# A front that reads x twice instead of turning and normalizing it, with 23 of 36 convolution taps as matmuls

## The chip, the cores and the metric

The kernel runs on one core of one Trainium2 chip. The metric is the device time of one execution in microseconds (us). Before the change three runs took 2659.55, 2660.99 and 2661.44 us; the median, 2660.99 us, is the time before.

## What is computed

Four layers follow each other on an image batch x of 2 x 512 x 32 x 32 in float32. The change touches the beginning of the first layer only, a deformable attention:

```python
xn = _bn(x, bn1_g, bn1_b)                       # x * s + b, per channel
q = _gconv1x1(xn, qw)                           # 8 groups of 64 channels
off = conv_general_dilated(qg, off_dw_w, (4, 4), ((1, 1), (1, 1)), ...)   # depthwise, 6 x 6 = 36 taps
off = gelu(off + off_dw_b)
off = tanh(einsum(off, off_pw_w)) * 4.0         # two offsets for each of 8 x 8 positions
vgrid_scaled = ...                              # positions moved by the offsets
kv = _grid_sample(xn, vgrid_scaled)             # bilinear samples, 0 outside the image
k = _gconv1x1(kv, kw)
v = _gconv1x1(kv, vw)
pos = grid_q - grid_kv                          # every pixel against every sampled position
bias = sign(pos) * log1p(abs(pos))
bias = relu(bias @ cpb_w1 + cpb_b1)             # 2 -> 128
bias = relu(bias @ cpb_w2 + cpb_b2)             # 128 -> 128
bias = (bias @ cpb_w3 + cpb_b3)                 # 128 -> 1
attn = softmax(qh kh + bias); out = attn vh     # then a projection, an MLP, and three more layers
```

There are 2 images x 8 groups of 64 positions and 1024 pixels. The kernel takes two groups (128 channels) at a time as a chunk k = 0..3, and one image of one chunk as g = 0..7. Position j of both groups of a g is a "key": 512 keys in all, n = 0..511.

## The kernel before

**Front (lines 367 to 618).** It loads x channel by channel into four tiles `xn[k]` (128 channels x 2048 pixels, 1 MB each) and makes everything that the first key needs. For chunk 0: `normed_` (VectorE) scales and shifts x, `query` (TensorE, line 421) multiplies by the query weights `qw`, `queried` (ScalarE, line 426) copies the result to `q` in another pixel order. 36 taps follow: 21 on VectorE (`Chain.tap`, lines 229 and 232) and 15 as matmuls with diagonal weights (`taps_pe`, lines 372 and 519; the diagonals are made on VectorE and GpSimd, line 451). Line 535 adds the two sums. Then `gelu`, `offsets`, `tanh`, `position`, `size`, `log`, `sign`, `feature` make a table of sign * log for the 64 positions; for the first eight keys matmuls spread it over all partitions (`pfb`, line 568) and `tab_scale` (line 174) makes the table `tab`. `turn`, `turned` and `put` store the table to DRAM (`fd`, line 331), from where `tab_load` (line 162) reads it for all later keys, eight at a time.

The same front also makes q for chunks 1 to 3 (`norm` on ScalarE or `normed_` on VectorE, `query`, `queried`), and turns the normalized x: `flip_x` (TensorE transposes, line 437) and `flipped` (copies, line 438) write it with pixels on partitions into `xt`, a view of the big tile `x`. The samples need it in that form.

**Order.** After `started.append(0)` every instruction that is wrapped in `pin` stays in program order on its engine. The order of the front is therefore written out by hand. Loads go out on SP's queue (`nc.sync`) and, at the start, on ScalarE's.

**Loop over keys (lines 972 to 985).** For each pair of keys p and each quarter o of 32 hidden units, `second` (line 649) runs eight matmuls into `ph`, one of two PSUM buffers, and ScalarE's relu (line 658) empties it. `first` (VectorE, line 355) makes the input `h1` of key n + 2, `combine` (VectorE, line 664) joins two quarters. `h1` has four buffers. All other work is put between these by a plan: `at(n, when, fn)` runs fn after quarter 0/2 or 1/3 of key n. `prepare(g)` samples: `hat`, `hat2` (ScalarE) and `cross` (VectorE) make bilinear weights from the coordinates `co`, `sample` (TensorE, line 738) multiplies them with `xt`, `got` (VectorE, line 749) copies the samples to `kv`. `attend(g)` does the softmax of an earlier g. `chain(k0, k1, n, taken)` repeats the front's work from the taps to `put` for chunk 1 (ending at key 85) and for chunks 2 and 3 together (ending at key 213), with all taps on VectorE.

Of the kernel before, what the change touches and what calls it, by code (L numbers as in the profile page):

```python
# [56 lines left out]
_CONSTS = [("ident", P), ("grid", 2 * J), ("gridf", J), ("npx", 1), ("npy", 8), ("sel3", 2)]  # L57
# [15 lines left out]
def conv_seq(  # L73
    ctx: ExitStack,
    tc: tile.TileContext,
    x_in: bass.AP,
    vecs: bass.AP,
# [24 lines left out]
    xt = x.rearrange("p k n -> p (k n)").rearrange("p (t c) -> p t c", c=C)  # L102
# [32 lines left out]
    with ExitStack() as ctx_l0:  # L135
# [66 lines left out]

        class Chain:
# [79 lines left out]

# [81 lines left out]
        with tc.tile_pool(name="a", bufs=1) as a, tc.tile_pool(name="aps", bufs=5, space=PSUM) as aps, tc.tile_pool(  # L367
            name="apc", bufs=1, space=PSUM
        ) as apc, tc.tile_pool(name="apk", bufs=1, space=PSUM) as apk:


            taps_pe = [(1, 2), (1, 3), (1, 4)] + [(ky, kx) for ky in (0, 5) for kx in range(6)]
            diag = a.tile([P, len(taps_pe), P], F32, name="diag")
            xn = [a.tile([P, NT], F32, name=f"xn{k}") for k in range(KC)]
            qw = a.tile([P, KC, P], F32, name="qw")
            ordc = a.tile([P, NORDER], F32, name="ordc")
            nc.scalar.dma_start(qw[:, 0], qkv_w[:, 0, 0])
            nc.scalar.dma_start(cst, consts)
            nc.scalar.dma_start(qw[:, 1:], qkv_w[:, 0, 1:])
            for t in range(NT // 512):  # L380
                b, half = divmod(t, 2)
                nc.sync.dma_start(xn[0][:, t * 512 : (t + 1) * 512], x_dram[0][:, b, half * 512 : (half + 1) * 512])
            for k in range(1, KC):
                nc.sync.dma_start(xn[k].rearrange("p (b n) -> p b n", b=B), x_dram[k])
                if k == 1:
                    nc.sync.dma_start(offw, off_w)
                    nc.sync.dma_start(cpbw, cpb_w)
                    nc.sync.dma_start(ordc, order)
            nc.sync.dma_start(kvw, qkv_w[:, 1:3])
            nc.sync.dma_start(wo, out_w)  # L390
            started.append(0)
            pqs, pts = {}, {}
# [4 lines left out]
            for _ in range(9):  # L397
                pin(nc.tensor.matmul(pidle, lhsT=idle, rhs=idle, start=True, stop=True))


            def norm(k):
                pin(
                    nc.scalar.activation(
                        xn[k], xn[k], AF.Identity, bias=v("L0_conv_bn1_b", k), scale=s12[:, 0, k : k + 1]
                    )
                )

            def normed_(k, *ts):
                for t in ts:
                    xs = xn[k][:, t * 512 : (t + 1) * 512]  # L410
                    pin(
                        nc.vector.tensor_scalar(
                            xs, xs, s12[:, 0, k : k + 1], v("L0_conv_bn1_b", k), ALU.mult, ALU.add
                        )
                    )

            def query(k, *ts):
                for t in ts:
                    pqs[k, t] = aps.tile([P, 512], F32, name="pq", tag="p")
                    rhs = xn[k][:, t * 512 : (t + 1) * 512]  # L420
                    pin(nc.tensor.matmul(pqs[k, t], lhsT=qw[:, k, :], rhs=rhs, start=True, stop=True))

            def queried(k, *ts):
                for t in ts:
                    pin(
                        nc.scalar.copy(
                            q[:, k, t * 512 : (t + 1) * 512].rearrange("p (y c x) -> p y c x", c=4, x=SIDE),
                            pqs.pop((k, t)).rearrange("p (y x c) -> p y c x", c=4, x=SIDE),
                        )
                    )  # L430

            def flip_x(k, t, copy):

                pt = aps.tile([P, 4, P], F32, name="pt", tag="p")
                for i in range(4):
                    at = (4 * t + i) * P
                    pin(nc.tensor.transpose(pt[:, i], xn[k][:, at : at + P], ident))
                pts[k, t] = lambda: pin(copy(xt[:, 4 * t : 4 * t + 4, k * P : (k + 1) * P], pt))

            def flipped(k, *ts):  # L440
                for t in ts:
                    pts.pop((k, t))()
# [9 lines left out]

            act, dve = nc.scalar.copy, nc.vector.tensor_copy
# [44 lines left out]
            ch = Chain(0, 1, lambda shape, name: apc.tile(shape, F32, name=name, tag="c"))  # L498
            for t in range(NT // 512):
                normed_(0, t)  # L500
                query(0, t)
                queried(0, t)
                if t == 1:
                    signs()
                elif t == 2:
                    diagonals(0, 2, nc.vector)
            diagonals(2, 7, nc.vector)
            diagonals(7, len(taps_pe), nc.gpsimd)
# [4 lines left out]
            flip_x(0, 0, act)  # L513
            flip_x(0, 1, act)
# [13 lines left out]
            flip_x(0, 2, act)  # L528
            flip_x(0, 3, act)
            flipped(0, 0, 1)  # L530
            norm(1)
            flipped(0, 2, 3)
            query(1, 0, 1, 2, 3)
            queried(1, 0, 1, 2)
# [3 lines left out]
            for i, m in enumerate(("below", "same")):  # L538
                pin(nc.tensor.matmul(pcnt[:, i : i + 1], lhsT=oc(m), rhs=pos, start=True, stop=True))
            ch.offsets()  # L540
# [3 lines left out]
            normed_(2, 0, 1)  # L544
            ch.position()
            flip_x(1, 0, act)
            flip_x(1, 1, act)
            ch.spread(0)
            flip_x(1, 2, act)
            flip_x(1, 3, act)  # L550
            ch.size()
            ch.log()
            ch.sign()
            normed_(2, 2)
            ch.coordinate(0)
            normed_(2, 3)
            ch.feature()
            counted()
            queried(1, 3)
            flipped(1, 0)  # L560

            tab0 = tabs[0] = tabp.tile([P, TK, 2, 64], F32, name="tab")
            for u0 in range(0, 8, 4):
                pfb = apk.tile([P, 4, 2, 64], F32, name=f"pfb{u0}")
                for u in range(4):
                    key = u0 + u
                    pin(
                        nc.tensor.matmul(
                            pfb[:, u].rearrange("p a f -> p (a f)"),
                            lhsT=ch.feat[:, key : key + 1].to_broadcast([P, P]),  # L570
                            rhs=ident,
                            start=True,
                            stop=True,
                        )
                    )
                for ax in range(2):
                    pin(tab_scale(tab0, ax, u0, u0 + 4, pfb))
                if u0 == 0:
                    flipped(1, 1, 2)
            first(0)  # L580
# [5 lines left out]
            flipped(1, 3)  # L586
            query(2, 0, 1)
            pw2 = apk.tile([P, P], F32, name="pw2", tag="pfb0")
            pin(nc.tensor.matmul(pw2, lhsT=cpbw, rhs=perm, start=True, stop=True))
            placed()  # L590
            first(1)
            norm(3)
            query(2, 2, 3)
            ch.spread(1)
            queried(2, 0, 1, 2, 3)
            psb = apk.tile([P, 4, 2], F32, name="psb", tag="pfb4")
# [3 lines left out]
            query(3, 0, 1)  # L600
            flip_x(2, 0, dve)
            query(3, 2)
            flip_x(2, 1, dve)
            query(3, 3)
            spread_out()
            ch.coordinate(1)
            queried(3, 0)
            flipped(2, 0)
            queried(3, 1, 2)
            flipped(2, 1)  # L610
            queried(3, 3)
            for k, t in ((2, 2), (2, 3), (3, 0), (3, 1), (3, 2), (3, 3)):
                flip_x(k, t, (dve, act)[t % 2])
            flipped(2, 2, 3)
            ch.column(0)
            flipped(3, 0, 1)
            ch.column(1)
            flipped(3, 2, 3)
# [8 lines left out]
        with tc.tile_pool(name="hid", bufs=3) as hid, tc.tile_pool(name="sm", bufs=1) as sm, tc.tile_pool(name="hps", bufs=2, space=PSUM) as hps, tc.tile_pool(  # L627
# [74 lines left out]
            def prepare(g):  # L702
# [28 lines left out]
                def sample():  # L731
                    pool, tag = (sps, "psim1") if own else (mps, "m")
                    ps = st["pkv"] = pool.tile([P, J], F32, name="pkv", tag=tag)
                    for t in range(8):
                        for h in range(2):
                            ch = k * P + h * DH
# [3 lines left out]
                                    lhsT=xt[:, b * 8 + t, ch : ch + DH],  # L740
# [6 lines left out]
                def got():  # L747
                    st["kv"] = smpp.tile([P, J], F32, name="kv")
                    pin(nc.vector.tensor_copy(st["kv"], st["pkv"]))
# [172 lines left out]

            def load(ch):
# [25 lines left out]
            def chain(k0, k1, n, taken):  # L949
                ch = Chain(k0, k1, lambda shape, name: mps.tile(shape, F32, name=name, tag="m"))  # L950
                for i, tap in enumerate(taps):
# [5 lines left out]
                    (10, 0, ch.sign), (11, 0, ch.feature), (11, 1, ch.column, 0), (12, 1, ch.column, 1),  # L957
                ]
                for i in range(k1 - k0):
                    plan += [(13 + i, 1, ch.turn, i), (14 + i, 0, ch.turned, i)]  # L960
                    plan += [(14 + i, 0, ch.put, i, b) for b in range(B)]
                for dn, when, fn, *args in plan:
# [3 lines left out]
            chain(2, 4, 213, 116)  # L966
# [1076 lines left out]
def _layout(a):  # L2043
# [46 lines left out]
    put("gridf", gq[:, None] + f(1.0) - f(2.0) / f(SIDE - 1) * gf)  # L2090
    put("npx", -(p % 32).astype(f)[:, None])
# [22 lines left out]
    for h in range(2):  # L2114
# [5 lines left out]
        "x": got["x"],  # L2120
        "vecs": vecs,
# [38 lines left out]
```

## Time and profile before

One execution was profiled. Its rows tell:

| what | value |
|---|---|
| the profiled execution's own time | 2659.79 us |
| its span, first to last instruction | 2658.0 us |
| around the span | 1.79 us |
| median of the three runs | 2660.99 us |
| front: span start to the first line-649 matmul | 37.38 us |
| matmuls of line 649, 16384 of them | 1770.7 us busy |
| relus of line 658, 1024 | 1141.8 us busy, 1115 ns each |
| `first` of line 355, 512 | 1169.3 us busy, 2284 ns each |
| `combine` of line 664, 512 | 653.9 us busy, 1277 ns each |
| VectorE, 37 to 787 us | 47.4 to 50.0 us busy in each 50 us |
| ScalarE, 37 to 787 us | 33.5 to 42.1 us busy in each 50 us |

A timeline row gives the start, the length, the engine, the line, the operation, "out<-in" by tile names, the shape, a count, and in brackets how long the engine had been idle and what ended it. Consecutive rows of one kind are merged, so the length of a row with x8 covers eight instructions. A float32 matmul appears as two passes, a transpose as one. In a row of stretches the busy time of each engine stands with the number of instructions, then the granted TensorE clock, the share of the DMA engines and GB/s.

### The profile page before, as it was taken

Reading aid. Unit: us, or ns where it says so; the run is one execution under the profiler, and the core shown is the slowest. Engines: PE = TensorE matmul, PEld = TensorE weight load, DVE = VectorE, ACT = ScalarE, POOL = GpSimd, SP = SyncE. Lnnn points to the kernel's source line nnn. Section 1 sums busy time; section 2 is a strip of 40 time slices with the busy share of each in tenths; the row PEclk is TensorE's granted clock in tenths of the full one; section 3 lists DMA queues with packets and bytes.
Section 4 is the critical chain, followed back from the end, with each engine's and each line's share of the span. In section 5 each row is a group of like instructions: output and inputs, shape, how many; then the busy total and the mean of one; then the engine's idle time right before and its main releaser. Section 6 shows DMA issues by size and latency. Waiting matters only on the chain.

```text
span 2658.0 us, 48892 instructions
## 1 busy us (share of the span) xinstructions
PE 2620.5 (99%) x19644; PEld 978.0 (37%) x19644; DVE 2252.6 (85%) x2042; ACT 1556.5 (59%) x2123; POOL 888.5 (33%) x1048
## 2 busy tenths in 40 slices
PE   9999999999999999999999999999999999999997
PEld 5222323333332333323232333333444444476544
DVE  7999999999999999999999999999554544648645
ACT  6777687777768777866867777777321111011334
POOL 1444444444444454444545445445200000000001
PEclk9999999999999999999999999999999999999998
DMA  4888888888888888888998899898410000010001
GB/s 138 167 165 170 167 157 161 173 159 161 172 167 157 160 178 157 164 174 160 172 199 172 158 194 177 159 177 158 101 31 24 16 24 24 16 65 1 1 1 64
DMA packets 113426, 335.08 MB, mean 126 GB/s; under 512 B 22672, under 2 KB 32400, under 8 KB 112432
## 3 DMA queue, kind: packets, MB, share of 16 engines
q0 software_dynamic: 77824, 251.72, 53.1%
q1 hardware_dynamic: 34800, 79.73, 9.0%
q8 instruction: 154, 2.52, 0.4%
q14 instruction: 72, 0.59, 0.1%
q10 hardware_dynamic: 576, 0.51, 0.1%
HBM read 58.99 MB, written 4.46 MB: 24 GB/s over the span
## 4 chain that ended last, share of the span: by engine, by line
PE 90%; DVE 5%; issue 2%; ACT 2%; DMA 0%; DVEq 0%; SPq 0%; ACTq 0%
PE ph L649 60%; PE A L1141 4%; PE D L1141 4%; PE C L1141 4%; PE B L1141 2%; PE po L1076 2%; DVE h L355 2%; DVE r L664 1%; PE pg L1339 1%; PE pscore L1649 1%; PE psim L692 1%; PE prC L1308 1%; PE prA L1308 1%; PE prD L1308 1%; PE pz L1678 1%
## 5 line engine op out<-in xcount | busy, mean ns | idle before, releaser
L649 PE MATMUL ph<-h,w2a 128*32 128x512 f32 x16384 | 1770.7, 592 | 7.5 <-ACT r L658 4.8
L658 ACT ACTIVATE r<-ph,sb 128x1024 f32<-128x1024 f32 x1024 | 1141.8, 1115 | 472.9 <-PE ph L649 453.2
L355 DVE CUSTOM_DVE_ANT_1 h<-tab 128x2048 f32<-128x2048 f32 x512 | 1169.3, 2284 | 19.1 <-PE ph L649 17.2
L649 PEld LDWEIGHTS ph<-h,w2a 128*32 128x32 f32 x16384 | 521.7, 109 | 1233.1 <-issue 769.3
L664 DVE SCALAR_TENSOR_TENSOR r<-r,rel,r 128x1024 f32<-128x1024 f32 x512 | 653.9, 1277 | 22.9 <-ACT r L658 21.6
L672 POOL DMA_DIRECT2D r<-r x512 | 473.4, 1141 | 175.5 <-DMA r<-r 164.8
L667 POOL DMA_DIRECT2D r<-r x256 | 234.7, 917 | 726.9 <-DVE r L664 617.0
L683 POOL DMA_DIRECT2D xs<-r x256 | 313.1, 1223 | 107.1 <-DMA xs<-r 83.6
L1423 POOL MEMSET M<- 128x512 f32 x2 | 1.0, 526 | 429.2 <-PE pt L1330 429.2
L174 ACT ACTIVATE tab<-tab,vec 128x256 f32<-128x256 f32 x252 | 137.6, 546 | 0.0
L1934 POOL TENSOR_TENSOR x<-x,aff 128x512 f32<-128x512 f32 x7 | 7.0, 1036 | 316.3 <-issue 316.3
L1181 ACT COPY u<-A 128x512 f32<-128x512 f32 x16 | 9.4, 586 | 146.9 <-PE A L1141 146.9
L1160 ACT ACTIVATE h<-h,vec 128x512 f32<-128x512 f32 x32 | 23.1, 721 | 113.7 <-DVE h L1163 113.7
L1163 DVE TENSOR_TENSOR h<-C,u 128x512 f32<-128x512 f32 x32 | 22.1, 690 | 48.6 <-PE C L1141 48.3
L1141 PE MATMUL A<-xn,w 128*128 128x512 f32 x128 | 60.3, 593 | 0.8 <-DVE x L1083 0.8
L1141 PE MATMUL C<-hT,w 128*128 128x512 f32 x128 | 60.3, 592 | 0.0
L1141 PE MATMUL A<-h,w 128*128 128x512 f32 x128 | 60.1, 592 | 0.0
L1201 DVE TENSOR_TENSOR x<-D,x 128x512 f32<-128x512 f32 x32 | 22.1, 690 | 25.8 <-PE D L1141 25.7
L1201 DVE TENSOR_TENSOR x<-C,x 128x512 f32<-128x512 f32 x32 | 22.1, 690 | 24.8 <-PE C L1141 24.8
L882 ACT ACTIVATE e<-e,den 128x64 f32<-128x64 f32 x128 | 42.4, 342 | 0.9 <-DVE den L878 0.9
L868 ACT ACTIVATE e<-psm,mx 128x64 f32<-128x64 f32 x128 | 39.3, 314 | 2.4 <-DVE mx L863 2.3
L1339 PE MATMUL pg<-xt 128*128 128x512 f32 (+3 forms) x128 | 36.4, 439 | 1.4 <-ACT xt L1337 1.1
(403 smaller groups left out, 1936.7 us busy)
## 6 DMA issues: line engine op xcount, KB each, us to landing
r<-r POOLq DMA_DIRECT2D x256, 512.0 KB, 5.0
r<-r POOLq DMA_DIRECT2D x256, 256.0 KB, 5.9
r<-r POOLq DMA_DIRECT2D x256, 128.0 KB, 4.7
tab<-fd SPq DMA_DIRECT2D x63, 512.0 KB, 6.4
xs<-r SPq DMA_DIRECT2D x256, 64.0 KB, 2.7
xs<-r POOLq DMA_DIRECT2D x256, 64.0 KB, 5.3
lw<-in_l_w_dram SPq DMA_DIRECT2D x5, 1024.0 KB, 9.0
x<-in_x_dram SPq DMA_DIRECT2D x4, 1024.0 KB, 12.2
```

The source lines that it names most:

```text
L174: return nc.scalar.activation(tf, tf if src is None else src[:, :, ax, :], AF.Identity, bias=0.0 if ax == 0 else v("L0_conv_cpb_b1"), scal ...
L355: nc.vector._custom_dve(TENSOR_ADD_SAT, out=h1, in0=columns.unsqueeze(1).to_broadcast([P, 32, 2, 32]), in1=rows_.unsqueeze(3).to_broadcast ...
L649: nc.tensor.matmul(ph[t * 32 : (t + 1) * 32, i, :], lhsT=w2a[:, o], rhs=h1s[2 * p + i][:, half * 16 : (half + 1) * 16, h, :], start=True, ...
L658: pin(nc.scalar.activation(r, ph, AF.Relu, bias=sb3[:, o, 1:2]))
L664: pin(nc.vector.scalar_tensor_tensor(r0, r1, rel[:, i : i + 1], r0, ALU.mult, ALU.add))
L667: pin(nc.gpsimd.dma_start(rs[p, 0], rs.pop((p, 2)), accum_op=ALU.add))
L672: pin(nc.gpsimd.dma_start(r[0 :: 2 * step], r[step :: 2 * step], accum_op=ALU.add))
L683: pin(nc.gpsimd.dma_start(xs_[t][d::8], rs.pop((p, 0))[4::8], accum_op=ALU.add))
L1076: nc.tensor.matmul(po, lhsT=(vwo, wo)[t // 2][:, k, o * P : (o + 1) * P], rhs=q[:, k, ts_], start=(k == 0), stop=(k == KC - 1),)
L1141: nc.tensor.matmul(banks[bank], lhsT=a[an][k], rhs=b_[bn_][k], start=(i < 4 and k == 0), stop=(k == n - 1), skip_group_check=True,)
L1308: nc.tensor.matmul(banks[bank], lhsT=a[an][:, k, o * P : (o + 1) * P], rhs=b_[bn_][:, k, :], start=(i < 4 and k == 0), stop=(k == 1), skip ...
L1339: nc.tensor.matmul(pgs[i], lhsT=xt[:, i * P : (i + 1) * P], rhs=xt[:, i * P :], start=(t == 0), stop=(t == 7),)
```

## The change

- x is not normalized. The scale goes into the query weights (`query_scale` makes `qws`), the shift becomes a bias of the query (`query_bias`: a one-column matmul for each chunk, copied to `qb`) that `queried` adds.
- x is not turned. A second input `x_pos` holds the raw x with pixels on partitions, laid out by the host; four loads of 1 MB put it into `xt`.
- So the samples are of raw x. `got` multiplies them by the scale and adds shift times the sum of the sample's weights, which is less than 1 at the image border. `off_middle`, `within` and `shifts` compute that sum, for all three chains.
- 23 taps instead of 15 run as matmuls; 9 diagonals are made on GpSimd, 8 on ScalarE and 6 on VectorE. VectorE keeps 13 taps.
- `size` and `sign` of the front's chain move to VectorE (`size_sign`, `signed`), the spreading matmuls become transposes, and the order of the front's instructions, the loads and the PSUM pools is new.

```diff
-            taps_pe = [(1, 2), (1, 3), (1, 4)] + [(ky, kx) for ky in (0, 5) for kx in range(6)]
+            taps_pe = [(1, kx) for kx in (2, 3, 4, 1, 0, 5)] + [(2, kx) for kx in (2, 3, 1, 0, 5)]
+            taps_pe += [(ky, kx) for ky in (0, 5) for kx in range(6)]
...
+            nc.scalar.dma_start(cst[:, 0:P], consts[:, 0:P])
             nc.scalar.dma_start(qw[:, 0], qkv_w[:, 0, 0])
-            nc.scalar.dma_start(cst, consts)
-            nc.scalar.dma_start(qw[:, 1:], qkv_w[:, 0, 1:])
...
+            nc.sync.dma_start(ordc, order)
+            nc.sync.dma_start(cpbw, cpb_w)
+            nc.sync.dma_start(cst[:, P:], consts[:, P:])
+            nc.sync.dma_start(offw, off_w)
+            nc.sync.dma_start(qw[:, 1:], qkv_w[:, 0, 1:])
             for k in range(1, KC):
                 nc.sync.dma_start(xn[k].rearrange("p (b n) -> p b n", b=B), x_dram[k])
...
+            nc.sync.dma_start(xt[:, 0].rearrange("p t c -> p (t c)"), x_pos[:, 0])
             nc.sync.dma_start(kvw, qkv_w[:, 1:3])
             nc.sync.dma_start(wo, out_w)
+            for k in range(1, KC):
+                nc.sync.dma_start(xt[:, k].rearrange("p t c -> p (t c)"), x_pos[:, k])
...
-            for _ in range(9):
+            for _ in range(6):
                 pin(nc.tensor.matmul(pidle, lhsT=idle, rhs=idle, start=True, stop=True))
...
+            query_bias(0, 1)
+            query_scale(0, nc.vector)
+            diagonals(6, 10, nc.scalar)
+            diagonals(14, len(taps_pe), nc.gpsimd)
+            diagonals(0, 4, nc.vector)
+            signs()
             for t in range(NT // 512):
-                normed_(0, t)
                 query(0, t)
                 queried(0, t)
...
+            query_bias(1, KC)
+            query(1, 0)
+            queried(1, 0)
             ch.offsets()
             ch.tanh()
...
+            query(1, 1, 2)
+            counted()
             ch.position()
+            ch.size_sign(a.tile([P, P], F32, name="sg"))
+            ch.log()
             ch.spread(0)
+            queried(1, 1)
+            ch.signed()
...
-                    pin(nc.vector.tensor_copy(st["kv"], st["pkv"]))
+                    pin(
+                        nc.vector.scalar_tensor_tensor(
+                            st["kv"], st["pkv"], s12[:, 0, k : k + 1], shift_of.pop(g), ALU.mult, ALU.add
+                        )
+                    )
...
+            for n, (fn, *args) in enumerate([(ch.off_middle, 1), (ch.within, 0), (ch.within, 1), (ch.shifts, 0)]):
+                at(n // 2, n % 2, fn, *args)
...
-                    (10, 0, ch.sign), (11, 0, ch.feature), (11, 1, ch.column, 0), (12, 1, ch.column, 1),
+                    (10, 0, ch.sign), (10, 1, ch.off_middle, 0), (11, 0, ch.feature), (11, 1, ch.column, 0),
+                    (12, 1, ch.column, 1),
...
+                m = 13 + k1 - k0
+                plan += [(m, 1, ch.off_middle, 1), (m + 1, 1, ch.within, 0), (m + 2, 0, ch.within, 1)]
+                plan += [(m + 3 + i, 1, ch.shifts, i) for i in range(k1 - k0)]
...
-            chain(2, 4, 213, 116)
+            chain(2, 4, 213, 110)
```

The new steps of a chain, each for all its columns (128 in the front's and chunk 1's chain, 256 in that of chunks 2 and 3):

```python
def off_middle(self, ax):      # two ScalarE instructions, 64 partitions each
    to = (self.acc, self.feat)[ax]
    for h in range(2):
        hs = slice(h * DH, (h + 1) * DH)
        pin(nc.scalar.activation(to[hs], co[hs, ax, h, self.cs], AF.Abs, bias=c("mid")[hs]))

def within(self, ax):          # two ScalarE instructions, the second reads the first
    t = (self.acc, self.feat)[ax]
    pin(nc.scalar.activation(t, t, AF.Relu, bias=c("mid")))
    pin(nc.scalar.activation(t, t, AF.Relu, bias=1.0, scale=-1.0))

def shifts(self, i):           # one VectorE instruction
    pin(nc.vector.scalar_tensor_tensor(to, self.acc[:, ks], b, self.feat[:, ks], ALU.mult, ALU.mult))
```

Between the spreading matmuls of the first four keys and those of the next four now stand `coordinate(0)`, `placed`, `first(0)`, one `query` and one `queried`; then come `turn`, `put`, `tab_load`, the four `psb` matmuls, `first(1)`, and the queries and copies of chunks 2 and 3, three of the copies on VectorE.

## The prediction

> **What bounds the kernel now.** I read the page first, for the bound of the whole:
>
> ```profile
> PE 2620.5 (99%) x19644; PEld 978.0 (37%) x19644; DVE 2252.6 (85%) x2042; ACT 1556.5 (59%) x2123; POOL 888.5 (33%) x1048
> L649 PE MATMUL ph<-h,w2a 128*32 128x512 f32 x16384 | 1770.7, 592 | 7.5 <-ACT r L658 4.8
> ```
>
> TensorE is busy throughout, mostly with line 649. So the front pays only through the moment S at which line 649 starts, and the loop pays for whatever stops it. TensorE's timeline of the front gives S = 37.38:
>
> ```profile
> 1.09 4.21 PE L398 MATMUL pidle<-idle 128*128 128x128 f32 x18 [1.09 <-DVE idle L395]
> ...
> 10.26 3.56 PE L519 MATMUL pacc<-q,diag 128*128 128x128 f32 x30
> ...
> 22.62 2.05 PE L568 MATMUL pfb<-cst,acc 128*128 128x128 f32 x16 [0.76 <-DVE acc L282]
> ...
> 33.92 2.78 PE L437 MATMUL pt<-cst,xn 128*128 128x128 f32 x24
> 37.38 13.94 PE L649 MATMUL ph<-h,w2a 128*32 128x512 f32 x128 [0.67 <-ACT x L438]
> ```
>
> From 22.62 on TensorE is never waiting long: it works off queries and turns, so its own instruction list sets S. Before that VectorE's taps do; its timeline:
>
> ```profile
> 10.61 7.69 DVE L232 SCALAR_TENSOR_TENSOR acc<-q,vec,acc 128x112 f32<-128x112 f32 x20
> 18.40 0.29 DVE L535 TENSOR_TENSOR acc<-acc,pacc 128x128 f32<-128x128 f32 x1
> ```
>
> TensorE's 15 taps were done by 13.82, VectorE's 21 only at 18.3.
>
> Third, ScalarE where the change puts new work into the loop: its timeline after S and, as stretches, after S and before key 232:
>
> ```profile
> 39.50 1.12 ACT L658 ACTIVATE r<-ph,sb 128x1024 f32<-128x1024 f32 x1 [2.17 <-PE ph L649]
> 40.51 0.68 ACT L714 ACTIVATE smp<-co,cst 128x128 f32<-128x128 f32 x2
> 41.10 1.11 ACT L658 ACTIVATE r<-ph,sb 128x1024 f32<-128x1024 f32 x1
> 42.10 0.68 ACT L714 ACTIVATE smp<-co,cst 128x128 f32<-128x128 f32 x2
> 42.81 1.11 ACT L658 ACTIVATE r<-ph,sb 128x1024 f32<-128x1024 f32 x1
> ```
>
> ```profile
> 39.50:52.50 13.00, 13.00 (x148) 4.44 (x144) 11.21 (x9) 12.72 (x20) 1.04 (x1) 1.00 0.16 30
> 851.50:873.00 21.50, 21.50 (x198) 6.10 (x194) 20.99 (x14) 21.36 (x41) 9.34 (x11) 1.00 0.83 157
> ```
>
> The fourth busy figure is ScalarE's: 59% over the span, but 98 and 99% here (and 20.82 of 21.20 from 387.6). In these stretches an added ScalarE instruction is not free.
>
> **Front, until q of chunk 0.** The first query now waits for the small weight load, then a one-column matmul, a copy and the scaling. That load landed 3.8 after its issue at 1.24; it is issued third now, at 1.67, so it lands near 5.6 (not before 5.04, where it landed before; not after 7.1, where the larger constants landed). The matmul 0.25 (line 539: four passes in 0.50), the copy 0.15, the scaling 0.28 and releases: first query at 6.6 instead of 5.3. Four queries at 0.86 (line 421: four passes in 1.88, the last 0.17 of it pipeline), the last copy 0.59: q is ready at 10.85, against 10.21 before. That is with TensorE at full rate. The idle passes took 0.234 each where later passes of 128 columns take 0.11, and the first query took from 5.30 to 6.65, so TensorE ran at half rate until some 6 us in, 4.9 us after its first pass. Now 12 idle passes end at 3.9 and a gap of two to three us follows. Full rate at once is one end (+0), half rate until about 13.5 the other (+3.5: 4 x 0.86 again). I take +1.0, between them, nearer the first end, as before's first query paid 0.5: q at 11.85.
>
> TensorE: Matmul & The Clock Gate, Part 1, of the Trainium skill speaks against this edit: only a busy window of about 3.4 us lifts the half clock, and the window runs free of the kernel. Before's row agrees (4.2 us of idle passes, all slow, though its clock column reads 1.00 there); 2.8 us of them may not fill a window, and by the rule alone the sum would have +1.5 to +3.5 here.
>
> **Taps to the first key's table.** 23 taps are 46 passes at 3.56/30 = 0.119: 5.46. VectorE's 13 at 0.385 (20 in 7.69): 5.0, so it is hidden behind TensorE now. The sum is added at 17.3 instead of 18.40. GpSimd's nine diagonals (5.43 for eight) end near 11.3, before tap 14 is due at 13.5. Then some is given back: TensorE runs pcnt (0.44), the biases of chunks 1 to 3 (six passes, 0.66), waits for their copy (0.35, since query(1,0) takes that PSUM buffer), and runs query(1,0) (0.86) ahead of `offsets`; queried(1,0) stands ahead of `tanh`. From the add to tanh 2.8 instead of 1.30: tanh at 20.1 instead of 19.70. From tanh to the first spreading the Ln table (1.28) and warm-up are as before, `counted` (11 VectorE instructions, 2.3) now stands ahead of `position` and costs 0.5, but the sign is on VectorE beside ScalarE's Ln, and a turn of x and a query no longer stand between: 2.3 instead of 2.92. pfb at 22.4 instead of 22.62.
>
> **pfb to S.** TensorE, in passes of 0.11 (128 columns) and 0.43 (512): pfb 4 + 4 as transposes 0.88, turn 0.11, psb 0.88, spread 0.44, nine queries 7.74: 10.05. S = 22.4 + 10.05 = 32.45. Before, this stretch took 14.76: gone are 32 turns (3.5), 8 passes of pfb (0.9), the pw matmul (0.2) and the waits for copies; one query more has come in. The first ph lies over buffers that the last copies don't use, so their 0.67 wait goes too. VectorE has first(0), first(1) done by 27 and its last copies by 31. **Gain at S: 37.38 - 32.45 = 4.9**; ends 6.8 (early weights, full rate) and 2.7 (half rate until 13.5).
>
> **Loads.** x_pos adds 4.19 MB ahead of the two `put`s and the `tab_load` on SP's queue. What was there ended by some 18.9:
>
> ```profile
> 6.00:11.00 5.00, 5.00 (x23) 2.69 (x21) 3.26 (x12) 3.18 (x6) 3.75 (x6) 1.00 1.04 393
> 11.00:16.00 5.00, 5.00 (x38) 4.28 (x37) 4.57 (x13) 3.62 (x5) 1.68 (x3) 1.00 1.03 417
> 16.00:18.75 2.75, 2.46 (x9) 1.18 (x8) 2.43 (x9) 1.37 (x4) 0.00 (x0) 1.00 1.06 435
> ```
>
> At 425 GB/s the new 4.19 MB end at 28.8. I let `put` wait for that end, the dear side (at once, it would land near 28): `put` 1.9, issue 0.6 and `tab_load` 4.6 after that: the second table lands near 36. It is needed by tab_scale after key 2's first quarter, 9.87 after S before (47.25), so at 42.3. I cost it at 0; 6 us cover it.
>
> DMA: Bandwidth & Descriptors (queues, rings and completion order) says that each engine's ring takes descriptors in order, so a small put cannot overtake megabytes queued before it. No row of before shows a put behind a long queue; by the rule the sum stays as it is.
>
> **Loop.** An Abs, Ln or Sign of 128 columns takes 0.29, the next independent one starts after 0.19 (21.95 to 22.14); of 256 columns 0.42 and 0.33. A pair where the second reads the first: 0.29 + 0.02 + 0.19 = 0.50, or 0.77.
> - Keys 0 and 1: off_middle 0.38, within twice 0.50: 1.38. All ahead of the hats, with ScalarE idle only 0.22 until 46.24. `second` two quarters later waits for the relu, `combine` too, and `cross` waits for hat2, and behind it `first` for key 4. The two ph buffers forgive 0.63 per lateness (1.74 a quarter less 1.11), of which some is used. I take 0.9.
> - Chunk 1, keys 95 to 101: two off_middle 0.76, within 1.00: 1.76, beside norm, hats and tab_scale. I take 1.3.
> - Chunks 2 and 3, keys 223 to 230: 1.32 + 1.54 = 2.86; 0.60 of idle before key 223 covers some. I take 1.9.
> - VectorE: four shifts at 0.2 (0.29 records), eight `got` at up to 0.07 more than the copy's 0.22 (nearest: 0.29 of a two-operand instruction): up to 1.4, but VectorE waits for ScalarE in these stretches. I take 0.2.
>
> Sum 4.3. Ends: 0, if ScalarE's other idle time takes it all, and 8.5, if every record counts in full.
>
> **Sum.** -4.9 + 4.3 = -0.6: the profiled execution would go from 2659.79 to 2659.2. It lay 1.2 below the median; for the median the prediction is 2660.99 - 0.6 = **2660.4**.
>
> **Rivals.**
> 1. The loop's additions are hidden, as ScalarE is idle for 473 us before relus. Against it: the two full stretches. Then only S counts: -4.9 + 0.2 = 2656.3, with TensorE at full rate from the first query 2655.3, and with early weights as well 2654.4.
> 2. Slower: the clock. If TensorE stays at half rate until 13.5, q is late by another 2.5, S = 34.95 and the gain is 2.4 against 4.3: 2662.9. It decides from S = 33.1, 0.65 above mine: 1.65 lost to the clock, so half rate until about 9.9 (half of the time from 6.6 on). For it: 18 passes at 0.234 before. Against: the queries themselves are TensorE work.
> 3. Slower: x_pos blocks the queue. If it moved at 160 GB/s, as DMA does in the loop, instead of 425, it would end at 45, the table land at 52, 9.9 after its need, and every us late is a us: 2670.3. It decides from an end of x_pos at 35. Against: 393 to 435 GB/s above.
>
> **How the numbers follow.** A measurement here can tell about 0.2% (5.3 us) from no change: below 2655.7 is faster, above 2666.3 slower. Forecast 0.42, own range 2657.5 to 2663.5; rival 1 0.27, over half of it below 2655.7 (0.16); rival 2 0.20, a third of it beyond 2666.3 if the loop costs its upper end too (0.07); rival 3 0.11, most of it slower (0.07). With the tails of the forecast (0.04 and 0.03): faster 0.20, same 0.63, slower 0.17. The range for 8 in 10 takes in rival 1 with early S and rival 2 with a dearer loop: 2654 to 2667.
>
> **What would show it.** First query at 6.6, q at 10.9 to 14.4 (the clock: lengths of line 519's and the first queries' passes); the add of pacc at 16.3 to 19.8; line 649 first at 31 to 35; fd's put landing near 31 and no wait of tab_scale at key 2; relus running late by over 0.6 at keys 0 to 3, 99 to 102 and 228 to 231, and TensorE's wait for them there. Wrong would be: S outside 30.5 to 35, or a loop longer by over 8.5 or shorter than before.

## The result, and the profile after

The changed kernel is slower: 2666.33 us against 2660.82 us (medians of 16 runs each), a ratio of 1.0021 with a 95% interval of 1.0013 to 1.0028. The forecast was 2660.4, 2654 to 2667. The profiled execution took 2666.58 us, its span 2664.8 us, 6.8 more than before's. Medians and intervals here and below are of the faster executions alone: one of the ten of e1_idle14 took 5649.88 us and is left out.

Two lines of the page answer to those shown of before (line 649 is 648 now):

```profile
PE 2620.0 (98%) x19590; PEld 972.7 (37%) x19590; DVE 2247.7 (84%) x2032; ACT 1557.4 (58%) x2140; POOL 888.1 (33%) x1049
L648 PE MATMUL ph<-h,w2a 128*32 128x512 f32 x16384 | 1772.8, 593 | 11.7 <-ACT r L657 8.8
```

The same work, 593 ns a matmul instead of 592; what grew is the idle time of TensorE ahead of it, 7.5 to 11.7, and ScalarE's relu is named for 8.8 of it instead of 4.8. TensorE's timeline of the front and the first keys:

```profile
1.09 2.93 PE L436 MATMUL pidle<-idle 128*128 128x128 f32 x12 [1.09 <-DVE idle L433]
6.61 0.56 PE L442 MATMUL pqb<-vec,qw 128*128 128x1 f32 x2 [2.60 <-DMA qw<-in_qkv_w_dram]
7.74 6.01 PE L459 MATMUL pq<-xn,qws 128*128 128x512 f32 x8 [0.57 <-DVE qws L453]
14.53 5.38 PE L544 MATMUL pacc<-q,diag 128*128 128x128 f32 x46 [0.78 <-ACT q L466]
...
24.90 0.65 PE L583 MATMUL pfb<-cst,acc 128*128 128x128 f32 x4 [0.38 <-DVE acc L294]
...
28.12 0.71 PE L323 MATMUL pc<-acc,cst 128*128 128x128 f32 x4 [0.38 <-ACT acc L360]
28.67 7.03 PE L459 MATMUL pq<-xn,qws 128*128 128x512 f32 x16
36.48 5.36 PE L648 MATMUL ph<-h,w2a 128*32 128x512 f32 x48 [0.78 <-ACT q L466]
42.16 1.92 PE L648 MATMUL ph<-h,w2a 128*32 128x512 f32 x16 [0.33 <-ACT r L657]
44.38 1.92 PE L648 MATMUL ph<-h,w2a 128*32 128x512 f32 x16 [0.29 <-ACT r L657]
46.83 5.36 PE L648 MATMUL ph<-h,w2a 128*32 128x512 f32 x48 [0.52 <-ACT r L657]
```

Eight passes for chunk 0 take 6.01, while sixteen of the same passes later take 7.03: TensorE ran at half rate for most of the 6.01 (before, with longer idle passes, the eight took 4.41 from 5.14). The taps are done 5.4 after they start, as they should be. But line 648 starts at 36.48, only 0.9 earlier than before, and is stopped three times in its first 10.4 us, where before 128 passes ran in one piece. ScalarE's timeline of that place:

```profile
38.59 1.11 ACT L657 ACTIVATE r<-ph,sb 128x1024 f32<-128x1024 f32 x1 [2.17 <-PE ph L648]
39.61 0.80 ACT L301 ACTIVATE acc<-co,cst 64x128 f32<-64x128 f32 x2
40.42 0.69 ACT L713 ACTIVATE smp<-co,cst 128x128 f32<-128x128 f32 x2
41.02 1.09 ACT L657 ACTIVATE r<-ph,sb 128x1024 f32<-128x1024 f32 x1
42.01 0.39 ACT L306 ACTIVATE acc<-acc,cst 128x128 f32<-128x128 f32 x1
42.44 0.31 ACT L307 ACTIVATE acc<-acc 128x128 f32<-128x128 f32 x1
42.65 0.68 ACT L713 ACTIVATE smp<-co,cst 128x128 f32<-128x128 f32 x2
43.24 1.09 ACT L657 ACTIVATE r<-ph,sb 128x1024 f32<-128x1024 f32 x1
```

Lines 301 (off_middle), 306 and 307 (within) stand between the relus, which start at 38.59, 41.02 and 43.24 instead of every 1.7. Stretches of the changed kernel (the busy times are of TensorE, its weight loads, VectorE, ScalarE and GpSimd; then the granted clock, the DMA share and GB/s):

```profile
38.59:52.50 13.91, 12.77 (x124) 3.45 (x118) 9.21 (x9) 13.70 (x26) 1.04 (x1) 1.00 0.07 14
...
856.00:880.00 24.00, 22.44 (x202) 5.78 (x198) 21.84 (x15) 23.90 (x48) 10.76 (x15) 1.00 0.86 165
```

```profile
2535.00:2545.00 10.00, 9.94 (x26) 5.44 (x27) 0.00 (x0) 1.56 (x3) 0.00 (x0) 0.84 0.00 0
```

ScalarE is full (13.70 of 13.91, 23.90 of 24.00), and TensorE, which had no gap there before, now has.

The last row, with a granted clock of 0.84, is a mean: taken in smaller steps, the clock reads 0.50 from 2534.9 to 2538.3. TensorE's timeline there, of the changed kernel and, after the dots, of the same instructions in the kernel before:

```profile
2535.06 1.94 PE L1679 MATMUL pt<-cst,e 128*128 128x128 f32 x8 [2.74 <-DVE e L1675]
...
2529.99 1.06 PE L1669 MATMUL pt<-cst,e 128*128 128x128 f32 x8 [2.74 <-DVE e L1665]
```

TensorE is idle for 2.74 in both, but in this one execution the passes behind it ran at half rate, and 1.6 of the 6.8 us arise there. The same gap of 2.74 stands in all eleven traces of this study, and in ten the eight passes took 1.06 or 1.07. The change adds nothing at this place, so the medians, 5.5 apart, are the better measure.

To see where the rest arises I took the times at which the psim matmuls start (at keys 46, 75, 110, ...). From line 648's start to key 75, from key 75 to 203, and from 203 to 238, before took 268.65, 463.57 and 133.76 us; the changed kernel 270.47, 465.56 and 136.07: **+1.8, +2.0, +2.3**, and nothing from key 238 to the end of the loop (970.94 both times). With -0.9 for the earlier start that is +5.2.

### The profile page after: what moved, and what is told of

It is laid out like the page before. It is cut to its first block, busy times and chain, and to the rows that moved or that the text cites. A ratio compares the mean times of both kernels' runs of the same rounds, so it can differ in the third digit from the quotient of the medians.

```text
span 2664.8 us, 48800 instructions
## 1 busy us (share of the span) xinstructions
PE 2620.0 (98%) x19590; PEld 972.7 (37%) x19590; DVE 2247.7 (84%) x2032; ACT 1557.4 (58%) x2140; POOL 888.1 (33%) x1049
## 4 chain that ended last, share of the span: by engine, by line
PE 87%; DVE 6%; ACT 3%; issue 3%; DMA 1%; POOL 0%; DVEq 0%; ACTq 0%; SPq 0%
PE ph L648 58%; PE A L1151 4%; PE D L1151 4%; PE C L1151 4%; PE B L1151 2%; PE po L1086 2%; DVE h L387 2%; DVE r L663 2%; PE pg L1349 1%; ACT r L657 1%; PE pscore L1659 1%; DMA r<-r 1%; PE pq L459 1%; PE psim L691 1%; PE pz L1688 1%
## 5 line engine op out<-in xcount | busy, mean ns | idle before, releaser
L648 PE MATMUL ph<-h,w2a 128*32 128x512 f32 x16384 | 1772.8, 593 | 11.7 <-ACT r L657 8.8
L682 POOL DMA_DIRECT2D xs<-r x256 | 320.2, 1251 | 116.8 <-DMA xs<-r 106.2
```

The source lines that it names most:

```text
L648: nc.tensor.matmul(ph[t * 32 : (t + 1) * 32, i, :], lhsT=w2a[:, o], rhs=h1s[2 * p + i][:, half * 16 : (half + 1) * 16, h, :], start=True, ...
L682: pin(nc.gpsimd.dma_start(xs_[t][d::8], rs.pop((p, 0))[4::8], accum_op=ALU.add))
```

## The experiments

All stand beside runs of the kernel before on the same chip. "First query" is its start and, after the slash, the span of the eight passes of chunk 0; "first tap" is VectorE's; S is the start of the loop's first matmul; the three losses are those just defined. All but the last column are from one trace each; those of e3_no_vector and e4_weights_first are of executions 2.8 and 2.2 us below the medians.

| run | first query | first tap | S | losses | time, ratio to before |
|---|---|---|---|---|---|
| before | 5.14 / 4.41 | 10.21 | 37.38 | 0, 0, 0 | 1 |
| changed | 7.74 / 6.01 | 14.51 | 36.48 | 1.8, 2.0, 2.3 | 2666.33, 1.0021 |
| e1_idle14 | 7.49 / 3.70 | 11.96 | 33.94 | 1.9, 2.0, 2.3 | 2662.74, 1.0011 (1.0001 to 1.0021) |
| e2_no_scalar | 7.29 / 6.38 | 14.44 | 36.41 | 0.1, 0.1, 0.0 | 2659.54, 0.9995 (0.9986 to 1.0005) |
| e3_no_vector | 7.27 / 5.40 | 13.42 | 35.39 | 1.9, 2.0, 2.3 | 2666.78, 1.0021 (1.0012 to 1.0031) |
| e4_weights_first | 6.34 / 5.43 | 12.54 | 34.51 | 1.8, 2.0, 2.4 | 2664.92, 1.0014 (1.0004 to 1.0023) |
| e5_placed | 7.74 / 6.33 | 14.82 | 36.79 | -0.4, 0.6, 0.5 | 2659.75, 0.9995 (0.9986 to 1.0005) |
| e6_all | 6.74 / 3.70 | 11.21 | 33.18 | -0.4, 0.6, 0.4 | 2656.34, 0.9983 (0.9974 to 0.9992) |
| e7_15taps | 7.21 / 5.40 | 13.36 | 39.17 | 1.8, 2.0, 2.3 | 2667.45, one run |
| e8_pools | 7.06 / 3.70 | 11.54 | 32.97 | -0.4, 0.6, 0.5 | 2655.71, one run |
| e9_spread | 6.28 / 3.70 | 10.95 | 32.38 | -0.4, 0.6, 0.5 | 2655.44, 0.9983 (0.9974 to 0.9992) |

### The clock at the start: e1_idle14

```diff
-            for _ in range(6):
+            for _ in range(14):
```

> The changed kernel with 14 idle matmuls instead of 6, so that TensorE has no gap between the idle passes (they ended at 4.0) and the first query weights (6.6). Theory (half clock): the eight query passes of chunk 0, 6.0 us in the changed kernel, take some 3.5, q is ready at 11.5 to 12.5 instead of 14.5, line 649 starts 2 to 3 earlier than 36.5, near 34, and the run is 2 to 3 us shorter. Rival (the queries wait for x or for the copies): the passes still span 6 us and nothing moves by over 0.5.

TensorE's timeline of this run:

```profile
1.09 5.72 PE L436 MATMUL pidle<-idle 128*128 128x128 f32 x28 [1.09 <-DVE idle L433]
6.64 0.28 PE L442 MATMUL pqb<-vec,qw 128*128 128x1 f32 x2
7.49 3.70 PE L459 MATMUL pq<-xn,qws 128*128 128x512 f32 x8 [0.56 <-DVE qws L453]
```

With no gap behind the idle passes, the queries take 3.70 instead of 6.01, though they start only 0.25 earlier. S comes 2.5 earlier, the time falls by 2.7 (by the two ratios) or 3.6 (by the medians), and the loop's losses stay. The rival, that queries wait for x or for copies, is out. In runs with six idle matmuls the span was 5.40, 5.40, 5.43, 6.01, 6.33 and 6.38. Half rate loses half of the time that it lasts, so by twice the excess over 3.70 the rate doubled 3.4 to 5.4 us after the first query started, between 9.8 (e4_weights_first) and 13.0 (e5_placed). That is my estimate; in e3_no_vector and e7_15taps it gives 10.7 and 10.6, and there the clock column goes from 0.50 to 1.00 at 10.9 and 10.8.

### ScalarE or VectorE in the loop: e2_no_scalar, e3_no_vector

```diff
# e2_no_scalar
-            ch.off_middle(0)
...
-            for n, (fn, *args) in enumerate([(ch.off_middle, 1), (ch.within, 0), (ch.within, 1), (ch.shifts, 0)]):
+            for n, (fn, *args) in [(3, (ch.shifts, 0))]:
...
-                    (10, 0, ch.sign), (10, 1, ch.off_middle, 0), (11, 0, ch.feature), (11, 1, ch.column, 0),
+                    (10, 0, ch.sign), (11, 0, ch.feature), (11, 1, ch.column, 0),
...
-                plan += [(m, 1, ch.off_middle, 1), (m + 1, 1, ch.within, 0), (m + 2, 0, ch.within, 1)]
```

> The changed kernel without off_middle and within in any chain (shifts then multiplies what lies in the tiles, so the border correction is left out); VectorE's shifts and got stay. Theory (ScalarE was full there): the loop's three losses against before, 1.8 after the start, 1.9 by key 110 and 2.3 by key 238, go to under 0.5 each, and the run is some 5 to 6 us shorter than the changed kernel, near before. Rival (VectorE's added work is the cost): the losses stay within 0.5 of what they are.

```diff
# e3_no_vector
-                plan += [(m + 3 + i, 1, ch.shifts, i) for i in range(k1 - k0)]
...
-                        nc.vector.scalar_tensor_tensor(
-                            st["kv"], st["pkv"], s12[:, 0, k : k + 1], shift_of.pop(g), ALU.mult, ALU.add
+                        nc.vector.tensor_scalar(
+                            st["kv"], st["pkv"], s12[:, 0, k : k + 1], v("L0_conv_bn1_b", k), ALU.mult, ALU.add
```

> The changed kernel without shifts, and with got as one scale and one shift per channel (the border correction is left out); ScalarE's off_middle and within stay. Theory (ScalarE): the loop's losses stay within 0.5 of 1.8, 1.9 and 2.3, except that at the start VectorE no longer waits for within ahead of cross, which may give back up to 0.5 more. Rival (VectorE): the losses fall by over 1 each.

Both kernels leave out the border correction. e2 also takes `off_middle(0)` out of the front; that moved nothing, from the first tap to S it has 21.97 like the changed kernel. Without ScalarE's steps the losses are 0.1, 0.1 and 0.0; without VectorE's they stay as they were. TensorE's first row in the loop of e2_no_scalar is in one piece again:

```profile
36.41 13.94 PE L647 MATMUL ph<-h,w2a 128*32 128x512 f32 x128 [0.78 <-ACT q L466]
```

So ScalarE's 22 small instructions in the loop cost the six microseconds and VectorE's four shifts and eight dearer `got`s nothing. The half microsecond that I allowed e3 at the start did not come: `cross` waits for hat2, which stands behind within on ScalarE, with or without shifts. The run e3 has its S 1.1 earlier than the changed kernel with the same front, by the clock and the landing of the weights alone (its first query started at 7.27 and took 5.40).

### The weights first: e4_weights_first

```diff
+            nc.scalar.dma_start(qw[:, 0], qkv_w[:, 0, 0])
             nc.scalar.dma_start(cst[:, 0:P], consts[:, 0:P])
-            nc.scalar.dma_start(qw[:, 0], qkv_w[:, 0, 0])
```

> The changed kernel with the first query weights loaded ahead of the identity on ScalarE's queue. Theory: they land near 5.1 to 5.6 instead of 6.6 and the identity about 1 later instead, the first query starts about 1 earlier than 7.74 and line 649 0.7 to 1.3 earlier, if the diagonals of ScalarE and GpSimd are still in time. Rival (what sets the start is the clock, not the weights): a query that starts earlier only runs longer at half rate, and line 649 moves by under 0.5.

The first query starts 0.9 to 1.4 earlier than in runs with the old order, and S comes 0.9 earlier than in e3, which has the same query span (5.43 and 5.40). So in these traces an earlier query was not paid back by the clock. Against the changed kernel's own trace the gain is 2.0, but e3 with the old order is already 1.1 ahead of that trace, so half of it is scatter. The medians are 1.4 below the changed kernel and 1.9 below e3, with intervals that overlap. The rival is unlikely but not excluded: there is one trace of each kernel, and the point at which the rate doubles moves by 3 us between them.

### The same steps at other keys: e5_placed

```diff
-            for n, (fn, *args) in enumerate([(ch.off_middle, 1), (ch.within, 0), (ch.within, 1), (ch.shifts, 0)]):
-                at(n // 2, n % 2, fn, *args)
+            for n, when, fn, *args in [(4, 1, ch.off_middle, 1), (5, 1, ch.within, 0), (6, 1, ch.within, 1), (7, 0, ch.shifts, 0)]:
+                at(n, when, fn, *args)
...
-                m = 13 + k1 - k0
+                m = 16 + k1 - k0
...
-            chain(1, 2, 85, 81)
-            chain(2, 4, 213, 110)
+            chain(1, 2, 85, 77)
+            chain(2, 4, 213, 106)
```

`got` of the first g moves from (4, 0) to (7, 1), and what follows it by as much.

> The changed kernel with its front as it is, but the loop's new ScalarE steps at keys where ScalarE was not full before: off_middle and within at keys 4 to 6 (with got and what follows three keys later), 102 to 104 and 231 to 233 instead of 0 and 1, 99 to 101 and 228 to 230; the taps of chunks 1 and 2 start four keys later. Theory (a ScalarE step costs only where ScalarE is full): the losses of 1.8, 1.9 and 2.3 fall to under 0.8 each, and the run is 3 to 5 us shorter than the changed kernel. Rival (the steps cost their length wherever they are): the losses stay above 1.3 each.

The losses are -0.4, 0.6 and 0.5, and the run is 6.6 us below the changed kernel: the same steps cost 6.1 at the old keys and 0.7 at the new ones, so their price was set by the key at which they ran more than by their length. Two stretches of this run, behind those that were full:

```profile
408.00:425.00 17.00, 17.00 (x178) 6.16 (x174) 16.25 (x11) 11.78 (x19) 8.72 (x12) 1.00 0.83 157
...
873.00:890.00 17.00, 16.90 (x174) 6.03 (x170) 16.22 (x11) 12.30 (x19) 10.53 (x13) 1.00 0.87 173
```

ScalarE is busy 11.78 of 17.00 and 12.30 of 17.00 there with the new steps in, and TensorE keeps going. The first loss is below zero; `got`, `project` and the rest of the first g were moved as well, and the taps of the two chains start four keys earlier, which may be why, but no run moved these alone.

### All three mends: e6_all, e9_spread, e8_pools

e6_all joins e4, e5 and 12 idle matmuls.

> The changed kernel with the first query weights loaded first, 12 idle matmuls and the loop's steps placed as in the run with placed steps: meant to beat both kernels. Theory: line 649 starts at 32.5 to 33.5 (37.38 before), the loop loses 0.5 to 2 in all, and the time is 2.5 to 4 us below before. If the gains of the start don't add up (the weights' landing and the clock overlap), line 649 starts near 34 and the gain is 1.5 to 2.5.

S is 33.18, 4.2 before the kernel before, the loop loses 0.6, and the time is 2656.34: faster than both kernels, by 0.17% (0.08 to 0.26%) than before. The weights' landing and the clock add up: S is 0.76 earlier than in e1_idle14, whose first query started 0.75 later.

Two things of the front still stood in the trace: `spread(1)` waits 0.38 for the turned copy (the 28.12 row above), and line 648's first matmul waits 0.78 for the last copy of a query. e9_spread is e6_all with `query(2, 0, 1)` ahead of `spread(1)`; e8_pools has that and the PSUM pools in before's order (aps, apc, apk).

> The run with all three mends, with spread(1) behind two of the queries: its wait of 0.38 on the turned copy (they share one PSUM buffer) should go, line 649 start 0.3 to 0.4 earlier than 33.2 if clock and weights fall as there, and the time be 0 to 0.5 us below that run's 2656.3. If the wait only moves (to coordinate(1) and the copies behind it), line 649 starts no earlier.

> The run with all three mends, with the front's PSUM pools in the order of before (the buffers of the queries first) and with spread(1) behind two of the queries. It asks why the first matmul of line 649 waits 0.78 for the last query's copy, which the prediction held to be gone. If the buffer ph lies over a query's buffer now and would lie over others with this order, the wait ends with another copy, or grows or goes by over 0.3. If the first ph needs all of the front's copies whatever the order, the wait stays 0.78. Moving spread(1) should take away its 0.38 wait on the turned copy.

TensorE's timeline of e9_spread:

```profile
24.04 1.96 PE L459 MATMUL pq<-xn,qws 128*128 128x512 f32 x4
25.84 0.61 PE L323 MATMUL pc<-acc,cst 128*128 128x128 f32 x4
26.29 5.32 PE L459 MATMUL pq<-xn,qws 128*128 128x512 f32 x12
32.38 4.07 PE L648 MATMUL ph<-h,w2a 128*32 128x512 f32 x36 [0.78 <-ACT q L466]
```

The 0.38 is gone: from pfb to S 11.05 instead of 11.58. In time it can't be told from e6_all (0.9983 both); part of the earlier S is an earlier landing of the weights. The 0.78 stayed, in e8_pools too, so the order of the pools does not set it. Which dependency makes the first ph wait for the front's last copy stays open.

### 15 taps instead of 23: e7_15taps

```diff
-            taps_pe = [(1, kx) for kx in (2, 3, 4, 1, 0, 5)] + [(2, kx) for kx in (2, 3, 1, 0, 5)]
-            taps_pe += [(ky, kx) for ky in (0, 5) for kx in range(6)]
+            taps_pe = [(1, 2), (1, 3), (1, 4)] + [(ky, kx) for ky in (0, 5) for kx in range(6)]
```

> The changed kernel with the 15 taps of before on TensorE and 21 on VectorE. Theory (VectorE's taps set the add before): from the first tap to the add 8.2 instead of 5.44, and line 649 2.2 to 2.8 later than with 23 taps, measured from the first tap. Rival (the copies and queries after it set line 649 anyway): the add comes 2.7 later, line 649 by under 1.

From the first tap to the add 8.0 instead of 5.4, as said; but S is 3.8 later from the first tap, 1.3 more than the taps; I had expected 2.2 to 2.8. TensorE's timeline and one stretch say why:

```profile
17.87 1.10 PE L458 MATMUL pq<-xn,qws 128*128 128x512 f32 x2
22.15 0.79 PE L254 MATMUL pf<-acc,offw 128*128 128x128 f32 x2 [3.17 <-ACT acc L249]
22.73 3.62 PE L458 MATMUL pq<-xn,qws 128*128 128x512 f32 x4
...
22.00:27.00 5.00, 4.85 (x10) 2.79 (x11) 2.62 (x13) 3.21 (x7) 0.00 (x0) 0.50 1.02 424
```

With fewer taps TensorE is idle for 3.17, and the four passes behind it take 3.62 instead of 1.88: the rate halved again, and the granted clock reads 0.50. From the add to `pfb` that made 1.1 of the 1.3. So the 23 taps are worth 2.6 by themselves and, in this one execution, another 1.3 by keeping TensorE at work.

## Why the prediction was wrong

It forecast -0.6 with no change as the likeliest reading; the measurement is +5.5, with both large terms off in the same direction. 2666.33 lies inside the range, at the corner that the text gave for it (the second rival's clock and a dearer loop), but S = 36.48 lies outside the 30.5 to 35 that it named.

- **q of chunk 0 at 11.85: wrong, 14.51.** This is the step that failed most, by 2.7. The first query was to start at 6.6 and started at 7.74: the weights landed 1.0 later than the 5.6 that I took (the upper bound 7.1 held), as they queue behind the identity (with the order turned round, in e4_weights_first, they landed at 5.3). And the term "half rate ... I take +1.0" was 2.3: the eight passes took 6.01, and 3.70 at full rate (e1_idle14). The second rival had this mechanism and its price; I gave it 0.20 and put my value nearer the kind end on the ground that before's query paid only 0.5, although before's idle passes ran on to its first query and the changed ones stop 2.6 short of the next matmul. e1_idle14 shows it: 3.70, S 2.5 earlier.
- **Taps, 5.45 from q to the add: right, 5.44.** VectorE's 13 taps are hidden, and e7_15taps confirms the 2.6.
- **The add to tanh 2.8, tanh to pfb 2.3: right, 2.58 and 2.37.**
- **pfb to S 10.05: 11.58.** The pass counts were right; the wait of spread(1) on a shared PSUM buffer (0.38) was missed, and the wait of the first ph for the last copy, which I held to be gone, is 0.78 as against 0.67 before.
- **Loads at no cost: right.** x_pos moved at 419 to 426 GB/s between 16 and 26 us. The puts went out from 28.1, while x_pos was still moving; once they had landed, the second table was asked for at 32.1 and landed 3.5 later, near the 36 forecast, and tab_scale of key 2 read it at 47.97; the third rival is out.
- **Loop +4.3: it was 6.1 (1.8, 2.0, 2.3), all of it on ScalarE.** The mechanism and the three places were right, the sizes too small. I priced Abs and Relu of 128 columns by the Abs, Ln and Sign rows (0.29, next start after 0.19). The new instructions with a bias read from a tile take 0.39 to 0.40, and behind `off_middle` the next starts after 0.40 (39.61 to 40.42 for two): the work was 2.1, 2.9 and 3.8 instead of 1.4, 1.8 and 2.9. I took 0.65, 0.74 and 0.66 of the work as its cost; the same shares of the measured work give 6.0 (an estimate). The hats, Abs of 128 columns with such a bias, showed 0.39 in the trace of before; that was the nearer row, though the next one starts after 0.29 there, and why it takes 0.40 behind `off_middle` no run shows. VectorE's 0.2 was 0.
- **The first rival (hidden work) is out for this order, and right for another:** e5_placed hides nearly all of it with the same instructions.

In sum the front missed by 4.0 (1.1 weights, 1.3 clock beyond the allowance, 1.5 the two waits and some tenths, 0.1 the rest) and the loop by 1.8. The ends given for the gain at S, 6.8 and 2.7, don't follow from the prediction's own terms, which give 6.5 (4.9 + 1.0 + 0.6) and 2.4 (4.9 - 2.5, as its second rival has it); the forecast doesn't rest on them.

## What to carry to other kernels

An engine with 40% idle time over the span can be full just where new work is put: read its busy time in the stretch of the step, and move the step by a few keys before giving up on it. Warm-up passes helped here only where they ran on to the first real work; when an edit delays that work, the warm-up has to grow with it. Price an instruction by the row with the same operands (a bias from a tile or none), not by the one with the same function and size.

## What the runs showed of the hardware

- **Half rate returns after a short gap, in some executions.** In e7_15taps TensorE's last pass ahead of the 3.17 us gap ended at 18.97, and the clock column reads 0.50 from 21.0 to 27.8. The gap of 2.74 us ahead of line 1679 did it in one of eleven traces. The 0.72 ahead of pf in the kernel before did not.
- **Warm-up takes unbroken work.** TensorE: Matmul & The Clock Gate (Part 1) of the Trainium skill gives about 3.4 us of sustained activity to raise the clock. Here the 5.72 us of idle passes in e1_idle14 contain the change, and 2.93 us followed by a gap of 1.3 to 2.6 were not enough in any of six traces. Where the clock column shows half rate ahead of the kernels' last 30 us, it lasts 3.4 (changed kernel, 2534.9 to 2538.3; e3_no_vector, 7.5 to 10.9; e7_15taps, 7.4 to 10.8) or twice that (e7_15taps, 21.0 to 27.8).
- **The clock column can miss half rate at the start.** It reads 1.00 in all eleven traces while the first idle passes take some 0.23 us each, where later ones take 0.11, and shows the slow queries only in e3_no_vector and e7_15taps, from 7.5 and 7.4 on; in the changed kernel and three others with the same slow queries it reads 1.00 throughout. There the length of the passes tells.
- **A ScalarE instruction with a bias from a tile is 0.08 to 0.10 longer.** The copies of a query went from 0.59 (Copy, line 426) to 0.69 (Identity with bias, line 466); within's two Relus of 128 columns, on the same tile, take 0.39 with the bias from a tile and 0.31 with a constant.
